# A modulated convolution chain on one core: VectorE's order in the first three quads is rearranged

## The chip, the cores and the metric

The kernel runs on one core of one Trainium2 chip. The metric is the device time of one execution in microseconds (us). In the profile PE is TensorE's matmul, PEld its weight load, DVE VectorE, ACT ScalarE, POOL GpSimd and SP SyncE, which issues most DMAs.

## The reference

The input x has 128 samples of 64 channels by 1024 positions; each sample has a style vector of 128. Four layers follow each other, with weights that depend on the sample, and x is added to the result:

```python
def _layer(x, style, w, b, mw, mb, typ):
    s = style @ mw.T + mb
    weight = SCALE * w * s[:, None, :, None]
    demod = lax.rsqrt(jnp.sum(weight * weight, axis=(2, 3)) + EPS)
    weight = weight * demod[:, :, None, None]
    if typ == 'same':          # 3-tap convolution
        out = jax.vmap(_conv_same)(x, weight) + b[None, :, None]
    elif typ == 'upsample':    # transposed convolution, stride 2, then a 4-tap blur
        out = jax.vmap(_conv_up)(x, weight.transpose(0, 2, 1, 3)) + b[None, :, None]
        out = _blur(out, 2.0 * blur_k, (1, 1))
    elif typ == 'downsample':  # 4-tap blur, then a convolution with stride 2
        xb = _blur(x, blur_k, (2, 2))
        out = jax.vmap(_conv_down)(xb, weight) + b[None, :, None]
    return out
...
for i, typ in enumerate(('same', 'upsample', 'same', 'downsample')):
    out = _layer(out, style, weights[i], biases[i], mod_w[i], mod_b[i], typ)
return x + out
```

No layer has a nonlinearity, so for each sample the four layers are one linear map of x plus a constant, apart from a few positions at both ends.

## The kernel before, in words

The kernel makes use of that. Four samples form a quad, and there are 32 quads. For each quad it first multiplies the layers' weights together and then convolves x with the product.

The weights of a quad pass through four steps on TensorE: `scale3` (ScalarE) and `stage1` (psS, L374) combine two layers, `stage2` (psR, L444) brings in the blur, `stage3` (psW, L485) the first layer. In the loop `stage1` is cut into `stage1_a` and `stage1_b`; `stage1_b` ends with VectorE at L427 and POOL at L430, which both write S. The result W is copied out of PSUM by ScalarE (L345), in the setup partly by VectorE (L347, the constant `BOTH`). `combine_a` and `combine_b` then make the sums H of W (L506) and add the residual to W (L503), all on VectorE.

The convolution itself is a fast convolution: five products, m = 0 to 4, of transformed inputs with transformed weights, each a group of 24 matmuls of 340 columns (`product`, L598). The inputs are made from x by VectorE and POOL, for a quad q:

- `in3` makes T3 from X (L556); `in_g01` and `in_g2` make the two parts of G from X (both L506, G01 with 1376 elements a row and G2 with 684), and after `in_g2` the buffer of X is free, so `load(q + 2)` follows and starts the DMA of quad q + 2 on SyncE's queue.
- `in1` and `in2` make T1 and T2 from G (L571, L576). They take the engine as an argument: in the loop it is POOL.
- `in04` makes T04 from G (L585). There is a single buffer of G, so the next quad's `in_g01` must come behind `in1`, `in2` and `in04` of this one.

The products are `conv3`, `conv1`, `conv2` and `conv0`, all in one PSUM tile psA, and `conv4` in the tile Y. `conv3` starts the bank; ScalarE copies it (`copy_m3`, L630). After `conv1`, VectorE's `sum1` makes y from psA (L506); `conv2` adds to the same bank and so waits for `sum1`. After `conv2`, `sum2` writes Y (L506) and y (L649), and `conv4` adds to Y, `conv0` to psA. ScalarE writes the three outputs (L667) and SyncE stores them.

A constant term runs beside this: `const_first(l)` is a small matmul into Y (L753), `const_rest(l)` turns it into cc or oc on VectorE (L765 to L770) for the next one.

Nothing schedules this kernel: the program is under a manual schedule, so each engine executes its instructions in the order in which the code issues them, and waits by semaphores for what it reads. The order around the change is written out by hand: a setup part for quads 0 and 1, and then a loop over q in which, with n = q + 1 and c = q + 2, the convolution of quad n starts, that of quad q ends, and the inputs of quad c are prepared (`in3(c)`, `in_g01(c)`, `in_g2(c)`, `load(c + 2)`, then `in1(c)`, `in2(c)` on POOL). A sample of the loop before, without what stands between:

```python
combine_a(n); combine_b(n); conv4(q)
...
in04(n); in3(c); in_g01(c)
...
in_g2(c); load(c + NX); extra(q, 1); sum1(n)
...
in1(c, nc_g); in2(c, nc_g); extra(q, 2)
```

`extra` runs small pieces of setup that belong to given quads; `slot` gives small matmuls a place in TensorE's queue.

Of the kernel before, what the change touches and what calls it, by code (L numbers as in the profile page):

```python
# [63 lines left out]
def kernel(  # L64
# [12 lines left out]
    NQ = B // 4  # L77
# [47 lines left out]
    NX = 2  # L125
# [77 lines left out]
    def mod_by_layer(bs, src, dst, f):  # L203

        for l in range(NL):
            nc_a.activation(
                dst[:, l, bs], by_layer(src, bs)[:, l], f, bias=mbs[:, l : l + 1], scale=SCALE
            )
# [255 lines left out]
    def stage3(q, part, pool=None, engs=(nc_a, nc_a)):  # L464

        rt = chain[q]
        ps = unit(pool or ps_w, f"psW{q}_{part}")
        if part == 0:
            Wq[q] = (
                wf_pool.tile([P, 2, K, K, C], F32, tag="Wf", name=f"Wf{q}"),  # L470
                wf_pool.tile([P, 3, 2, K, C], F32, tag="H", name=f"H{q}"),
            )
        W = Wq[q][0]
        kinds = ((0, 1), (2,))[part]
        n = 0
        for i, kind in enumerate(kinds):
            for k in range(K):
                gs = [g for g in range(K) if 0 <= K * g + kind - k < 7]
                lo, m = gs[0], len(gs)
                first = K * lo + kind - k  # L480
                n += 1
                for r, rows in enumerate(HALF):
                    for c, cols in enumerate(HALF):
                        at = (K * i + lo) * C
                        nc.tensor.matmul(  # L485
                            ps[r][cols, at : at + m * C],
                            w0s[kind][rows, k, :],
                            rt[c][rows, first : first + K * (m - 1) + 1 : K, :],
                            start=(n == 1),
                            stop=(n == K * len(kinds)),  # L490
                            skip_group_check=True,
                        )
        for r in range(2):
            dst = W[:, r, kinds[0] : kinds[-1] + 1].rearrange("c t g o -> c (t g o)")
            scaled_copy(engs[r], dst, ps[r][:, : len(kinds) * K * C], t0[:, q, r : r + 1])
        return ps
# [56 lines left out]
    def in3(q, pairs=BOTH_PAIRS):  # L553
        if q < NQ:
            X, t = Xs[q % NX], t_tile(q, "T3")
            nc_v.tensor_sub(t[:, pairs, 0, :NJ], plane(X, 3, pairs), plane(X, 1, pairs))  # L556

    def in_g01(q, pairs=BOTH_PAIRS):
        if q < NQ:
            X, g = g_tile(q)  # L560
            sum_of(g[:, pairs, PL:], X[:, pairs, : 2 * PL], 0.5, X[:, pairs, PL:], ALU.subtract)

    def in_g2(q, pairs=BOTH_PAIRS):
        if q < NQ:
            X, g = g_tile(q)
            sum_of(plane(g, 2, pairs), plane(X, 3, pairs), 0.5, plane(X, 2, pairs), ALU.subtract)
# [65 lines left out]
    def conv1(q, *groups):  # L632
        product(q, 1, banks(q), groups or range(K))

    def sum1(q):

        y1w[q] = m_tile("y1", q, 2)
        for s, a in parts(q):
            sum_of(y1w[q][:, s], a, 2.0, m3c[q][:, s])
# [14 lines left out]
    def conv0(q, *groups):  # L654
        product(q, 0, banks(q), groups)
# [85 lines left out]
    def const_of(l, bs):  # L741

        n = bs.stop - bs.start
        at = NB + 4 + l * n
        return Y[:, 0, at : at + n]
# [4 lines left out]
    def const_first(l, bs):  # L750
        src = c0f if l == 0 else cc[l - 1]
        for cols in HALF:
            nc.tensor.matmul(  # L753
                const_of(l, bs)[cols],
                wsum[T, l, :],
                src[T, bs],
                start=False,
                stop=True,
                skip_group_check=True,
            )  # L760

    def const_rest(l, bs, src):
        src = src[:, : bs.stop - bs.start]
        if l == 2:
            nc_v.tensor_mul(oc[:, bs], src, dm[:, 3, bs])  # L765
            nc_v.tensor_scalar(oc[:, bs], oc[:, bs], bb[:, 3:4], None, op0=ALU.add)
        else:
            add, f = ((b1s, 2.0), (c2f, 1.0))[l]
            nc_v.tensor_mul(cc[l][:, bs], src, (a1, Da)[l][:, bs])
            nc_v.scalar_tensor_tensor(  # L770
                cc[l][:, bs], add[:, bs], f, cc[l][:, bs], op0=ALU.mult, op1=ALU.add
            )
# [221 lines left out]
    weight_sums(1, 2)  # L994
    stage1(1, ps_conv)
    in_g01(0, PAIR[1])
    stage3(0, 0, None, BOTH)
    in3(0)
    stage3(0, 1, ps_conv, BOTH)
    const_first(0, first)  # L1000
    stage1(2)
# [8 lines left out]
    stage2(1, ps_conv)  # L1010
    conv3(0)
    copy_m3(0)
    const_first(1, PART[0])
    in04(0)
    const_rest(1, PART[0], const_of(1, PART[0]))
    stage3(1, 0)
    mod_by_layer(LATER, raw[0][:, 0], sc, AF.Identity)
    in3(1)
    conv1(0)
    in_g01(1, PAIR[0])  # L1020
    in_g01(1, PAIR[1])
    const_first(2, PART[0])
    sum1(0)
    const_rest(2, PART[0], const_of(2, PART[0]))
    in_g2(1)
    load(1 + NX)
    table_b(first)
    in1(1, nc_g)
    in2(1, nc_g)
    for of in (table_B, vector_a1, table_0, vector_b1, vector_c2):  # L1030
        of(PART[1])
    table_Bn(slice(0, PART[1].stop))
# [71 lines left out]
    for q in range(NQ):  # L1104
        n, c, s = q + 1, q + 2, q + 3
        if q == 1:
            nc.sync.dma_start(Xe, x_ends)
        if n == NQ:
            for i, queue in enumerate((nc.sync, nc_a)):
                output(q, 1, i, nc_v)  # L1110
                store(q, i, slice(1, 2), queue)
            conv4(q)
            for i in range(2):
                output(q, 2, i)
                store(q, i, slice(2, K))
            conv0(q, *range(K))
            for i, (eng, queue) in enumerate(zip(BOTH, (nc_a, nc.sync))):
                output(q, 0, i, eng)
                store(q, i, slice(0, 1), queue)
            break  # L1120
        if c < NQ:
            stage2(c)
        if n < NQ - 1:
            sum2(q)
        if n < NQ - 1:
            combine_a(n)
            combine_b(n)

        if n == NQ - 1:

            conv3(n, ps_w)
            copy_m3(n)
            conv4(q, 0, 1)
            for i in range(2):
                output(q, 1, i)
            conv1(n)
            sum1(n)
            conv4(q, 2)
            for i in range(2):
                output(q, 2, i)  # L1140
                store(q, i, slice(1, K))
            in04(n, PAIR[0])
            in04(n, PAIR[1])
            conv0(q, 0)
            conv2(n)
            conv0(q, 1, 2)
            sum2(n)
            for i in range(2):
                output(q, 0, i)
                store(q, i, slice(0, 1))  # L1150
            continue

        conv4(q)
        if q == 0:
            var_matmul(PART[1], var_of(PART[1]), start=False)
            var_root(PART[1], var_of(PART[1]))
            var_newton(PART[1])
            table_A(PART[1], dm[:, 2, PART[1]])
            for of in (table_C, vector_c0, table_3, vector_Da):
                of(PART[1])  # L1160
        for i in range(2):
            output(q, 2, i)
        if c < NQ:
            stage3(c, 0)
        conv3(n)
        copy_m3(n)
        extra(q, 0)
        in04(n)
        in3(c)
        in_g01(c)  # L1170
        if c < NQ:
            stage3(c, 1)
        conv0(q, 0)
        conv1(n, 0)
        if q in SLOTS:
            slot(*SLOTS[q])
        elif s < NQ:
            stage1_a(s)
        conv1(n, 1, 2)
        for i in range(2):  # L1180
            output(q, 1, i)
        in_g2(c)
        load(c + NX)
        extra(q, 1)
        if n == NQ - 2:
            combine_a(n + 1, lambda: sum1(n))
            combine_b(n + 1)
        else:
            sum1(n)
        conv0(q, 1)  # L1190
        if q in SLOTS:
            stage1_a(s)
        elif s < NQ:
            stage1_b(s)
        conv0(q, 2)
        for i in range(2):
            output(q, 0, i)
        conv2(n, 0)
        if q in SLOTS:
            stage1_b(s)  # L1200
        if c < NQ - 1:
            in1(c, nc_g)
            in2(c, nc_g)
        extra(q, 2)
        if s + 1 < NQ:
            scale3(s + 1)
        conv2(n, 1, 2)
        if n == NQ - 2:
            sum2(n)
            in1(n + 1, nc_v)  # L1210
            in2(n + 1, nc_v)
        for i in range(2):
            store(q, i)
# [74 lines left out]
```

## Time and profile before

| What | us |
|---|---|
| median of 3 timed runs | 488.8 |
| lowest and highest of them | 488.52, 490.86 |
| the profiled execution, its own time | 488.43 |
| span of its trace | 486.6 |
| TensorE matmul busy | 478.0 |
| VectorE busy | 381.0 |
| ScalarE busy | 289.9 |
| GpSimd busy | 140.8 |

The span runs from the first to the last instruction of the trace; the execution's own time holds 1.83 us more. Times within the trace count from the start of the span. The loop's first iteration begins at about 33 us, its second at 48 us, and one iteration takes 14 to 15 us. A row of the timeline gives the start, the duration, the engine, the line, the operation, the tile written and the tiles read, and how many instructions are merged; brackets at its end give how long the engine stood idle before it, and what ended that.

### The profile page before, as it was taken

The numbers are of one execution on the slowest core, as the hardware profiler recorded it, in microseconds if no ns is written. First come the engines' busy times: TensorE is split into PE (matmuls) and PEld (weight loads), VectorE is DVE, ScalarE is ACT, GpSimd is POOL, SyncE is SP. The second block draws the span as 40 slices with busy tenths as digits, with TensorE's granted clock in tenths as the row PEclk, the third lists the DMA queues.
The fourth block names the chain that finished last, engine by engine and source line by source line (L and its number), as shares of the span: only waits on it lengthen the run. The fifth ranks groups of instructions, "written<-read, shape, count | busy, mean of one in ns | idle before, by whom it ended". The sixth has DMA issues, their size and how long they took to land.

```text
span 486.6 us, 22180 instructions
## 1 busy us (share of the span) xinstructions
PE 478.0 (98%) x10048; PEld 366.9 (75%) x10048; DVE 381.0 (78%) x630; ACT 289.9 (60%) x579; POOL 140.8 (29%) x173
## 2 busy tenths in 40 slices
PE   8979999999999999999999999999999999999996
PEld 7957777767777777778887877768887777888863
DVE  4787887887798868977867988758888786988784
ACT  5447556666656656656656556656656666556553
POOL 2448035432325333113322123322123331213300
PEclk9989999999999999999999999999999999999999
DMA  7132534444334543344542344442344542244224
GB/s 246 48 145 74 196 128 177 175 157 154 104 118 172 176 176 106 111 153 160 175 166 68 123 173 176 175 141 73 140 175 175 176 173 102 98 174 175 90 87 174
DMA packets 20303, 70.42 MB, mean 145 GB/s; under 512 B 2288, under 2 KB 3824, under 8 KB 20208
## 3 DMA queue, kind: packets, MB, share of 16 engines
q1 hardware_dynamic: 19840, 68.53, 39.4%
q8 instruction: 79, 1.29, 1.0%
q10 hardware_dynamic: 368, 0.46, 0.3%
q14 instruction: 16, 0.13, 0.1%
HBM read 35.36 MB, written 33.62 MB: 142 GB/s over the span
## 4 chain that ended last, share of the span: by engine, by line
PE 96%; DVE 3%; issue 0%; DVEq 0%
PE psA L598 45%; PE psR L444 16%; PE psW L485 14%; PE Y L598 11%; PE psS L374 5%; PE psE L829 2%; PE Y L169 1%; PE Y L321 1%; DVE G L506 1%; DVE H L506 0%; PE psM L193 0%; DVE T L585 0%; DVE T L556 0%; DVE Wf L347 0%; DVE T L571 0%
## 5 line engine op out<-in xcount | busy, mean ns | idle before, releaser
L598 PE MATMUL psA<-T,H 64*64 64x340 f32 x2304 | 193.9, 448 | 2.1 <-DVE y L506 2.0
L598 PEld LDWEIGHTS psA<-T,H 64*64 64x64 f32 x2304 | 96.2, 133 | 51.9 <-issue 13.6
L430 POOL TENSOR_TENSOR S<-S 128x128 f32<-128x128 f32 x29 | 13.7, 471 | 290.9 <-ACT S L345 290.9
L444 PE MATMUL psR<-S,E 64*64 64x192 f32 (+1 forms) x2304 | 87.3, 300 | 0.0
L444 PEld LDWEIGHTS psR<-S,E 64*64 64x64 f32 x2304 | 81.1, 134 | 7.4 <-issue 0.6
L345 ACT ACTIVATE R<-psR,tC 128x448 f32<-128x448 f32 x63 | 36.5, 630 | 72.7 <-PE psR L444 72.7
L506 DVE SCALAR_TENSOR_TENSOR G<-X 128x1376 f32<-128x1376 f32 (+2 forms) x66 | 76.2, 1193 | 0.0
L598 PE MATMUL psA<-T,Wf 64*64 64x340 f32 x768 | 74.7, 447 | 0.0
L345 ACT ACTIVATE Wf<-psW,t 128x384 f32<-128x384 f32 (+1 forms) x126 | 56.3, 497 | 10.9 <-PE psW L485 10.8
L485 PE MATMUL psW<-R,w0s 64*64 64x128 f32 (+1 forms) x1536 | 61.8, 287 | 0.0
L598 PE MATMUL Y<-T,Wf 64*64 64x340 f32 x768 | 61.7, 446 | 0.1
L506 DVE SCALAR_TENSOR_TENSOR Y<-m,psA 128x680 f32<-128x680 f32 (+1 forms) x33 | 28.0, 850 | 37.2 <-PE psA L598 36.7
L485 PEld LDWEIGHTS psW<-R,w0s 64*64 64x64 f32 x1536 | 51.5, 133 | 6.7
L585 DVE TENSOR_TENSOR T<-G 128x1368 f32<-128x1368 f32 (+1 forms) x33 | 50.8, 1542 | 0.1
L506 DVE SCALAR_TENSOR_TENSOR y<-psA,m 128x680 f32<-128x680 f32 (+1 forms) x33 | 27.8, 844 | 28.9 <-PE psA L598 28.4
L667 ACT ACTIVATE o<-Y,tb,td 128x340 f32<-128x340 f32 x64 | 37.1, 630 | 21.4 <-ACT R L345 16.8
L571 POOL TENSOR_TENSOR T<-G 128x684 f32<-128x684 f32 x30 | 49.8, 1660 | 0.1
L576 POOL TENSOR_TENSOR T<-G 128x684 f32<-128x684 f32 x30 | 49.5, 1650 | 0.0
L374 PEld LDWEIGHTS psS<-wd,w2n 64*64 64x64 f32 x1160 | 39.4, 133 | 10.0
L667 ACT ACTIVATE o<-psA,tb,td 128x340 f32<-128x340 f32 x63 | 36.6, 633 | 14.7 <-PE psA L598 14.7
L598 PEld LDWEIGHTS Y<-T,Wf 64*64 64x64 f32 x768 | 33.6, 133 | 14.8 <-issue 0.6
L506 DVE SCALAR_TENSOR_TENSOR H<-Wf 128x384 f32<-128x384 f32 x64 | 39.6, 619 | 0.0
(145 smaller groups left out, 524.5 us busy)
## 6 DMA issues: line engine op xcount, KB each, us to landing
X<-in_x SPq DMA_DIRECT2D x64, 516.0 KB, 4.4
out<-o SPq DMA_DIRECT2D x60, 510.0 KB, 5.3
out<-o SPq DMA_DIRECT2D x6, 170.0 KB, 3.2
out<-o SPq DMA_DIRECT2D x2, 340.0 KB, 2.9
Xe<-in_x_ends SPq DMA_DIRECT2D x1, 512.0 KB, 6.8
par<-in_params SPq DMA_DIRECT2D x2, 192.0 KB, 3.3
out<-o ACTq DMA_DIRECT2D x2, 170.0 KB, 2.6
par_s<-in_params_s SPq DMA_DIRECT2D x1, 196.0 KB, 2.7
```

Source lines behind the costliest of these rows:

```text
L345: nc_a.activation(dst, src, AF.Copy, scale=f)
L374: nc.tensor.matmul(ps[r][cols, at * C : (at + n) * C], weight[rows], wd[c if r == 0 else 1 - c][rows, taps], start=first, stop=last, skip_ ...
L430: nc_g.tensor_add(t[:, :, 2], t[:, :, 2], t[:, :, 0])
L444: nc.tensor.matmul(ps[r][cols, lo * C : (lo + m) * C], E[rows, e + 2, :], src[rows, a, :], start=(n == 0), stop=(n == 8), skip_group_check ...
L485: nc.tensor.matmul(ps[r][cols, at : at + m * C], w0s[kind][rows, k, :], rt[c][rows, first : first + K * (m - 1) + 1 : K, :], start=(n == 1 ...
L506: nc_v.scalar_tensor_tensor(out, x, f, y, op0=ALU.mult, op1=op)
L571: eng.tensor_add(t[:, :, 0, :NJ], plane(g, 2), plane(g, 1))
L576: eng.tensor_sub(t[:, :, 1, :NJ], plane(g, 2), plane(g, 1))
L585: nc_v.tensor_sub(t[:, pairs, :, :NJ], both(a, PL), both(b, 1))
L598: nc.tensor.matmul(ps[s][cols, :NB], w, Ts[q, tag][rows, c, i, g : g + NB], start=(g == 0 and m == 3), stop=(g == K - 1), skip_group_check ...
L667: nc_a.activation(dst, src, AF.Identity, bias=add, scale=d3)
L829: nc.tensor.matmul(ps[r][cols, : HB * n].rearrange("c (b j) -> c b j", j=n), weight(i, r, c)[rows], moving(i, r, c)[rows], start=(i == 0), ...
```

## The change

Only the order in which instructions are issued changes, and the engine of four of them; every sum and every matmul stays. In the setup `in3(0)` moves ahead of `stage3(0, 0)`, and so ahead of VectorE's part in copying W of quad 0; `const_rest(1)` moves ahead of `in04(0)`; `sum1(0)` moves ahead of `in3(1)` and `in_g01(1)`, which is issued for both pairs at once in place of two halves. `in_g2(1)` and `load(3)` move into the first iteration of the loop, behind `combine_b(1)`. In the first iteration `in1(1)` and `in2(1)` run on VectorE ahead of `in04(1)`; `in3(2)` moves behind `sum1(1)`, and `in_g01(2)` behind `stage1_b(3)`. In the second iteration `in_g2(2)` and `load(4)` come ahead of `combine_a(2)`, `in1(2)` and `in2(2)` run on VectorE ahead of `in04(2)`, and `in_g2(3)` and `load(5)` move behind `stage1_b(4)`, with `in1(3)` and `in2(3)` on POOL as before. From the third iteration on the order is the old one.

```diff
     in_g01(0, PAIR[1])
+    in3(0)
     stage3(0, 0, None, BOTH)
-    in3(0)
     stage3(0, 1, ps_conv, BOTH)
...
-    const_first(1, PART[0])
+    const_first(1, first)
+    const_rest(1, first, const_of(1, first))
     in04(0)
-    const_rest(1, PART[0], const_of(1, PART[0]))
     stage3(1, 0)
     mod_by_layer(LATER, raw[0][:, 0], sc, AF.Identity)
+    conv1(0)
+    const_first(2, first)
+    sum1(0)
     in3(1)
-    conv1(0)
-    in_g01(1, PAIR[0])
-    in_g01(1, PAIR[1])
-    const_first(2, PART[0])
-    sum1(0)
-    const_rest(2, PART[0], const_of(2, PART[0]))
-    in_g2(1)
-    load(1 + NX)
+    const_rest(2, first, const_of(2, first))
+    in_g01(1)
     table_b(first)
-    in1(1, nc_g)
-    in2(1, nc_g)
...
         if n < NQ - 1:
+            if q == 1:
+                in_g2(n)
+                load(n + NX)
             combine_a(n)
             combine_b(n)
+            if q == 0:
+                in_g2(n)
+                load(n + NX)
...
+        if q < 2:
+            in1(n, nc_v)
+            in2(n, nc_v)
         for i in range(2):
             output(q, 2, i)
...
         in04(n)
-        in3(c)
-        in_g01(c)
+        if q:
+            in3(c)
+            in_g01(c)
...
-        in_g2(c)
-        load(c + NX)
+        if q > 1:
+            in_g2(c)
+            load(c + NX)
         extra(q, 1)
...
             sum1(n)
+        if q == 0:
+            in3(c)
         conv0(q, 1)
...
             stage1_b(s)
-        if c < NQ - 1:
+        if q == 0:
+            in_g01(c)
+        if q == 1:
+            in_g2(c)
+            load(c + NX)
+        if q and c < NQ - 1:
             in1(c, nc_g)
             in2(c, nc_g)
         extra(q, 2)
```

## The prediction

> **What bounds the kernel now.** I read the page first, then what ended TensorE's waits, then the stretches in which TensorE is not full, then the instructions there.
>
> ```profile
> span 486.6 us, 22180 instructions
> PE 478.0 (98%) x10048; PEld 366.9 (75%) x10048; DVE 381.0 (78%) x630; ACT 289.9 (60%) x579; POOL 140.8 (29%) x173
> PE 96%; DVE 3%; issue 0%; DVEq 0%
> PE psA L598 <- DVE y L506: 2.0, 1, 2.0
> PE Y L753 <- DVE cc L770: 0.6, 1, 0.6
> ```
>
> TensorE is busy for 478.0 of 486.6 us and the chain that ended last is 96% its own. No order of VectorE's work can shorten the matmuls. What such an order can change is TensorE's waits, and the last two rows are the only ones after the start that VectorE causes: 2.0 us for y (`sum1`) and 0.6 us for cc (`const_rest`). The next rows show that these two cost more than their length. Columns: stretch, its length, then busy time of PE, PEld, DVE, ACT and POOL, and the granted clock third from the end.
>
> ```profile
> 24.11:27.53 3.42, 2.81 (x64) 1.64 (x59) 3.32 (x6) 2.16 (x6) 0.00 (x0) 1.00 0.56 223
> 27.53:30.94 3.41, 1.45 (x34) 0.84 (x29) 3.38 (x7) 2.68 (x8) 0.37 (x1) 1.00 0.03 7
> 30.94:34.36 3.42, 3.42 (x44) 2.09 (x40) 1.46 (x3) 0.06 (x1) 3.26 (x4) 0.50 0.58 181
> ```
>
> From 30.94 to 34.36 TensorE never stops, but it has half its clock, so 3.42 us there hold 1.71 us of work. The stretch before it, of the same length, was only 1.45 us busy; the one before that, 2.81 us busy with the 0.6 us wait in it, was followed by full clock. I therefore read the half clock as the second cost of the 2.0 us wait. Together: 0.6 + 2.0 + 1.7, some 4.3 us, is all that there is to gain.
>
> The instructions around the two waits (start, duration, engine, line):
>
> ```profile
> 17.16 0.62 DVE L347 TENSOR_SCALAR Wf<-psW,t 128x384 f32<-128x384 f32 x1 [1.82 <-PE psW L485]
> 21.82 0.87 DVE L571 TENSOR_TENSOR T<-G 128x684 f32<-128x684 f32 x1
> 24.26 0.86 DVE L576 TENSOR_TENSOR T<-G 128x684 f32<-128x684 f32 x1
> 25.04 1.57 DVE L585 TENSOR_TENSOR T<-G 128x1368 f32<-128x1368 f32 x1
> 25.77 0.74 PE L598 MATMUL psA<-T,H 64*64 64x340 f32 x8
> 26.54 0.17 DVE L769 TENSOR_TENSOR cc<-Y,Da 128x16 f32<-128x16 f32 x1
> 26.91 0.87 DVE L556 TENSOR_TENSOR T<-X 128x684 f32<-128x684 f32 x1
> 27.13 0.23 PE L753 MATMUL Y<-cc,wsum 64*64 64x16 f32 x2 [0.61 <-DVE cc L770]
> 27.24 0.99 PE L485 MATMUL psW<-R,w0s 64*64 64x128 f32 x22
> 27.70 1.65 DVE L506 SCALAR_TENSOR_TENSOR G<-X 128x688 f32<-128x688 f32 x2
> 29.27 0.86 DVE L506 SCALAR_TENSOR_TENSOR y<-psA,m 128x680 f32<-128x680 f32 x1
> 30.18 2.99 PE L598 MATMUL psA<-T,H 64*64 64x340 f32 x24 [1.96 <-DVE y L506]
> 31.74 1.63 POOL L571 TENSOR_TENSOR T<-G 128x684 f32<-128x684 f32 x1
> 33.22 0.87 DVE L506 SCALAR_TENSOR_TENSOR Y<-m,psA 128x680 f32<-128x680 f32 x1 [1.96 <-PE psA L598]
> 34.77 0.61 DVE L506 SCALAR_TENSOR_TENSOR H<-Wf 128x384 f32<-128x384 f32 x1
> 36.13 1.90 PE L598 MATMUL Y<-T,Wf 64*64 64x340 f32 x24
> 38.83 0.22 DVE L234 TENSOR_SCALAR var<-Y 128x64 f32<-128x64 f32 x1 [0.78 <-ACT dm L233]
> 40.24 1.60 DVE L585 TENSOR_TENSOR T<-G 128x1368 f32<-128x1368 f32 x1
> 42.80 0.82 PE L598 MATMUL psA<-T,H 64*64 64x340 f32 x8
> ```
>
> `conv1(0)` ends at 25.77 + 0.74 = 26.51, so `sum1(0)` could start there. VectorE starts it at 29.27, because T04(0), cc, T3(1) and both halves of G01(1) stand ahead. `conv2(0)` writes the bank that `sum1(0)` reads and starts at 30.18, 0.05 after y is done. (T1, T2, T3, T04 are outputs of `in1`, `in2`, `in3`, `in04`; G01 and G2 of `in_g01`, `in_g2`.)
>
> **Part by part.** In the built program the queues of TensorE and ScalarE keep their order; VectorE gets four instructions that POOL loses (T1 and T2 of quads 1 and 2). So TensorE's pieces keep their lengths, and it is enough to run VectorE's new queue against them.
>
> T3(0) ahead of the copy of W: 0.87 us go into the 1.82 us in which VectorE waits for that copy's matmuls. Cost nothing; at 17.8 the next copy follows at once, and everything up to T2(0) moves up by about 0.67 us. TensorE is full until 26.51, so this gains nothing by itself; without that idle time it would cost nothing there either, as the old place cost the same.
>
> cc of quad 1 ahead of T04(0): T2(0) now starts at 24.26 - 0.67 = 23.59, cc is done near 24.8, before TensorE asks at 26.5. The 0.61 us wait goes. What is late next: T04(0) runs 24.85 to 26.42, and its readers come after 36 in the old run.
>
> `sum1(0)` ahead of T3(1) and G01(1): it starts when `conv1(0)` ends, 26.55, and ends at 27.41; `conv2(0)` starts at 27.46. The piece before it, psW, ended at 27.24 + 0.99 = 28.23 and is now 0.61 earlier, 27.62, its last matmul overlapping the next by about 0.2: no wait is left, or one of 0.1. So `conv2(0)` moves from 30.18 to 27.46, **2.72 us**. With full clock, 1.71 us more until the matmuls into Y: 36.13 becomes 31.70, a shift of **4.43 us**.
>
> Now what was put off. VectorE starts its next instruction about 0.08 before an independent one ends (T04 at 25.04 with 1.57, then cc at 26.54), so T3, T1, T2 and G2 take 0.78 each, G01 1.51. From `sum1(0)` at 26.55: 0.79, T3(1) 0.78, the two constants 0.35, G01(1) 1.51 reach 29.98, where `sum2(0)` begins; `conv2(0)` is done at 29.2, so that is 0.8 late, but its reader needs Y at 31.70 and it is there at 30.85. Y and y take 1.55 (33.22 to 34.77), H near 3.2 (3.11 between two rows of quad 1 below, a little more here), G2(1) 0.78: 35.5. Variances and the table take 1.41 (38.83 to 40.24): 36.94. T1(1) then ends at 37.81 on VectorE. Its first matmuls, at 42.80, are due at 38.37: 0.56 to spare, the thinnest cover in quad 0; if it is gone, its lack is the price, bounded by the 0.78 of T1. T2(1) and T04(1) end at 40.07, and `sum1(1)` must wait for its matmuls until 41.04.
>
> The load of quad 3 follows G2(1), so it is issued at 35.6, and it is needed at the T3(3) near 53: no price. Loads 4 and 5 are read later still.
>
> Quad 1 has the tightest stretch, from `sum1(1)` to `sum1(2)`:
>
> ```profile
> 45.47 0.87 DVE L506 SCALAR_TENSOR_TENSOR y<-psA,m 128x680 f32<-128x680 f32 x1 [0.53 <-PE psA L598]
> 46.26 0.61 DVE L427 SCALAR_TENSOR_TENSOR S<-psS,tB,S 128x128 f32<-128x128 f32 x2
> 48.49 0.87 DVE L506 SCALAR_TENSOR_TENSOR Y<-m,psA 128x680 f32<-128x680 f32 x1 [1.63 <-PE psA L598]
> 50.05 0.55 DVE L506 SCALAR_TENSOR_TENSOR H<-Wf 128x384 f32<-128x384 f32 x1
> 53.16 1.58 DVE L585 TENSOR_TENSOR T<-G 128x1368 f32<-128x1368 f32 x1
> 54.65 0.87 DVE L556 TENSOR_TENSOR T<-X 128x684 f32<-128x684 f32 x1
> 55.43 2.37 DVE L506 SCALAR_TENSOR_TENSOR G<-X 128x1376 f32<-128x1376 f32 x2
> 58.10 0.17 DVE L769 TENSOR_TENSOR cc<-raw,a 128x16 f32<-128x16 f32 x1 [0.30 <-ACT raw L688]
> 59.11 0.87 DVE L506 SCALAR_TENSOR_TENSOR y<-psA,m 128x680 f32<-128x680 f32 x1 [0.63 <-PE psA L598]
> 60.52 0.79 PE L598 MATMUL psA<-T,H 64*64 64x340 f32 x8
> ```
>
> Before, this stretch held waits of 1.63, 0.30 and 0.63 us. After, VectorE has no pause in it: y 0.79, T3(2) 0.78, S 0.53, G01(2) 1.51, Y and y 1.56, G2(2) 0.78, H 3.11 (50.05 to 53.16), T1(2) and T2(2) 1.56, T04(2) 1.49, T3(3) 0.78, G01(3) 1.51, cc 0.39: 14.79, then y 0.87 and the 0.05 of release, 15.71. TensorE reaches `conv2(2, 0)` 60.52 - 45.47 = 15.05 after `sum1(1)` starts, and that matmul overwrites what `sum1(2)` reads. So a **new wait of 0.66 us** stands there. Within the stretch S is done 0.6 before its reader and H in time; T1(2) ends near 51.0, due at 52.6. Afterwards G2(3) is behind S and is covered by the wait for S; quad 2 ends this backlog in its own slack, and from quad 3 on the order is the old one.
>
> T1 and T2 on VectorE are priced by 0.87 of the row at 21.82, the same operation on VectorE; the other bound is POOL's 1.63. I take 0.87, the engine's own row.
>
> Sum: 2.72 + 1.71 - 0.66 = 3.77 us. The profiled execution took 488.43 for its 486.6 of span and becomes 484.66; the median of the three timed runs is 0.37 above it, so I forecast 488.8 - 3.8 = 485.0.
>
> One rule bears on the 1.71. The half clock lasted 3.42 us after a stretch that was 1.45 of 3.41 busy and whose longest pause was 1.96. The Trainium skill, "TensorE: Matmul & The Clock Gate", in Part 1 and in "HAM oscillation", has the clock halve after at least one idle window of about 3.4 us, and advises against idle gaps above that; the length agrees with the trace, but here 1.96 us of pause was already followed by half clock. By the page's gap rule the wait would not be the cause, and the half clock could stay.
>
> **Rivals.** *The half clock stays, or comes back in quad 1.* For it: only one such event is in the trace, so its threshold lies anywhere between 1.45 and 2.81 busy us. Against it: with a pause of 0.66 at least 2.75 of 3.41 us are busy, next to the 2.81 that was harmless. It would leave 2.72 - 0.66 = 2.06: 486.7 us. The gap rule of the page gives this rival.
>
> *VectorE becomes the bound in quad 1, and the kernel is slower.* Its stretch of 15.71 us has no pause, so whatever stretches its instructions lengthens TensorE's wait one for one. At 2 us more the wait is 2.7, longer than the one that preceded the half clock; 1.71 follows, and the 4.43 is used up: that is the point of decision. With T1 and T2 at POOL's price (+0.78 each) and the five H operations as slow as this one was while POOL worked beside it (+0.34 each), it is 0.66 + 3.26 + 1.71, and some 0.35 in quad 0: 6.0 lost against 4.43, 490.4 us.
>
> ```profile
> 64.31 0.89 DVE L506 SCALAR_TENSOR_TENSOR H<-Wf 128x384 f32<-128x384 f32 x1
> ```
>
> Against it: VectorE's own T1 row, and POOL has little to do in that stretch once T1(2) and T2(2) are gone.
>
> *The change hides everything:* VectorE a little quicker than summed, no wait in quad 1: 4.4 saved, 484.4 us. It is the good end of the forecast and needs 0.66 us out of 15.71.
>
> **How the numbers follow.** No change, for a measurement of this kernel, is within 0.5%, 2.4 us. The forecast with its good end gets 0.80, all of it faster. The half clock that stays saves 2.06, under the bound, and with other half-losses that I cannot name gets 0.14. The slower rival gets 0.06. The range runs from 483.8 (the good end, less 0.6, somewhat more than the 0.37 by which two figures of the kernel before differ) to 487.0 (the half clock that stays, and 0.3): it leaves out little more than the slower rival.
>
> **What would show it.** In the changed profile: no wait for cc or y near 27 to 30, `conv2(0)` near 27.5, granted clock 1.00 from 27 to 38, TensorE's Y matmuls of quad 0 at 31.7, T1(1) on VectorE done near 37.8, one wait of TensorE for y of 0.3 to 1.2 us near 56, and from there the old timeline 3.8 us earlier. I am wrong if the clock is still 0.50 somewhere before 60, if TensorE waits for T or S in quad 0, or if the wait in quad 1 is above 1.5 us.

## The result, and the profile after

| | before | changed |
|---|---|---|
| median, us | 488.62 (7 runs) | 486.01 (7 runs) |
| lowest to highest, us | 487.43 to 490.86 | 485.38 to 486.75 |
| ratio of changed to before | | 0.9945, 95% interval 0.9926 to 0.9964 |

The changed kernel is 2.6 us faster (1.8 to 3.6 by the interval); 3.8 were forecast. The profiled execution took 486.4 us, its span is 484.6.

From the page of the changed kernel:

```profile
span 484.6 us, 22175 instructions
PE 476.6 (98%) x10048; PEld 373.4 (77%) x10048; DVE 384.6 (79%) x633; ACT 289.8 (60%) x579; POOL 133.9 (28%) x169
PE 91%; DVE 6%; DMA 1%; issue 0%; ACT 0%; DVEq 0%; ACTq 0%
```

What TensorE waited for in it (total, times, longest):

```profile
PE Y L169 <- DVE Z L142: 1.2, 1, 1.2
PE psA L598 <- DVE y L506: 0.7, 2, 0.5
```

The wait for cc is gone, and in place of one wait of 2.0 us for y there are two of 0.7 together. The chain shows more VectorE than before: from 22.5 to 57.7 us, in quads 0 and 1, VectorE now has one pause above 0.2 us, of 1.82 us ahead of `sum1(1)`.

The same stretches as before, with the granted clock third from the end:

```profile
24.11:27.53 3.42, 3.36 (x77) 2.46 (x68) 3.32 (x6) 2.18 (x7) 0.00 (x0) 1.00 0.56 226
27.53:30.94 3.41, 3.25 (x68) 2.40 (x72) 3.38 (x6) 2.72 (x8) 1.92 (x3) 1.00 0.01 2
30.94:34.36 3.42, 3.42 (x84) 2.57 (x80) 3.35 (x8) 1.21 (x3) 2.20 (x8) 1.00 0.02 5
```

TensorE is nearly full in all three, and there is no half clock. Its pieces, one row for each place where the prediction gave a time:

```profile
27.69 1.95 PE L598 MATMUL psA<-T,H 64*64 64x340 f32 x24 [0.22 <-DVE y L506]
...
31.95 1.90 PE L598 MATMUL Y<-T,Wf 64*64 64x340 f32 x24
...
35.58 1.97 PE L598 MATMUL psA<-T,H 64*64 64x340 f32 x24
37.67 1.29 PE L485 MATMUL psW<-R,w0s 64*64 64x128 f32 x22
...
39.32 0.94 PE L598 MATMUL psA<-T,H 64*64 64x340 f32 x8
...
57.71 0.80 PE L598 MATMUL psA<-T,H 64*64 64x340 f32 x8 [0.46 <-DVE y L506]
```

| start of | before | forecast | after | shift |
|---|---|---|---|---|
| `conv2(0)` | 30.18 | 27.46 | 27.69 | -2.49 |
| `conv4(0)` | 36.13 | 31.70 | 31.95 | -4.18 |
| `conv1(1, 0)` | 42.80 | 38.37 | 39.32 | -3.48 |
| `conv2(2, 0)` | 60.52 | 56.75 | 57.71 | -2.81 |

So 4.18 us were won by the matmuls into Y, a little under the forecast; 0.70 were lost between `conv4(0)` and `conv1(1, 0)`, which the prediction does not have; and 0.67 in quad 1, which it has as 0.66. From there on the two timelines keep a distance of 2.8 us (matmuls into psR at 207.54 and 204.73), and of 3.0 at the start of the last group of matmuls (480.13 and 477.13). What follows that group, the last stores, took about 1 us longer in this execution, so the span shows 2.0.

Where the 0.70 went: ScalarE, VectorE and the weight loads of the changed kernel near 36 us.

```profile
35.68 0.22 DVE L234 TENSOR_SCALAR var<-Y 128x64 f32<-128x64 f32 x1
...
35.99 1.16 ACT L667 ACTIVATE o<-Y,tb,td 128x340 f32<-128x340 f32 x2 [1.37 <-DVE var L234]
...
37.04 1.05 ACT L345 ACTIVATE Wf<-psW,t 128x384 f32<-128x384 f32 x2
...
37.67 0.20 PEld L485 LDWEIGHTS psW<-R,w0s 64*64 64x64 f32 x4 [0.72 <-ACT Wf L345]
```

ScalarE's first output waits 1.37 us for L234, a small VectorE instruction that reads the variances from the same bank of Y. Behind the output in ScalarE's queue stands the copy of W, and TensorE's next weights wait for that. In the kernel before the same output had waited 0.35 us for L234:

```profile
39.15 1.16 ACT L667 ACTIVATE o<-Y,tb,td 128x340 f32<-128x340 f32 x2 [0.35 <-DVE var L234]
```

The output uses nothing that L234 writes, so the wait is not for its result. The Trainium skill, "PSUM — Partial Sum Buffer", in "PSUM bank collisions raise a hardware error", says that ScalarE and VectorE must not read the same bank and quadrant at once, and that such accesses are put in an order; that fits the wait, and no run here tries it without.

### The profile page after: what moved, and what is told of

Its sections match the earlier page's. It is cut to its first block, busy times and chain, and to the rows that moved or that the text cites. A ratio compares the mean times of both kernels' runs of the same rounds, so it can differ in the third digit from the quotient of the medians.

```text
span 484.6 us, 22175 instructions
## 1 busy us (share of the span) xinstructions
PE 476.6 (98%) x10048; PEld 373.4 (77%) x10048; DVE 384.6 (79%) x633; ACT 289.8 (60%) x579; POOL 133.9 (28%) x169
## 4 chain that ended last, share of the span: by engine, by line
PE 91%; DVE 6%; DMA 1%; issue 0%; ACT 0%; DVEq 0%; ACTq 0%
PE psA L598 43%; PE psR L444 15%; PE psW L485 14%; PE Y L598 11%; PE psS L374 5%; PE psE L829 2%; DVE H L506 1%; DVE G L506 1%; DMA par_s<-in_params_s 1%; DVE T L585 1%; PE Y L321 1%; DVE T L556 0%; PE psM L193 0%; DVE T L571 0%; DVE T L576 0%
## 5 line engine op out<-in xcount | busy, mean ns | idle before, releaser
L598 PEld LDWEIGHTS psA<-T,H 64*64 64x64 f32 x2304 | 99.7, 133 | 47.1 <-issue 12.3
L506 DVE SCALAR_TENSOR_TENSOR G<-X 128x684 f32<-128x684 f32 (+1 forms) x65 | 76.1, 1206 | 0.0
L485 PE MATMUL psW<-R,w0s 64*64 64x128 f32 (+1 forms) x1536 | 62.8, 287 | 0.2
L485 PEld LDWEIGHTS psW<-R,w0s 64*64 64x64 f32 x1536 | 52.5, 133 | 6.8 <-ACT Wf L345 1.0
L571 POOL TENSOR_TENSOR T<-G 128x684 f32<-128x684 f32 x28 | 46.5, 1659 | 2.3 <-DVE G L506 2.3
L576 POOL TENSOR_TENSOR T<-G 128x684 f32<-128x684 f32 x28 | 46.5, 1661 | 0.0
L598 PEld LDWEIGHTS Y<-T,Wf 64*64 64x64 f32 x768 | 34.9, 133 | 13.7 <-issue 0.6
L345 ACT ACTIVATE S<-psS,tBn 128x256 f32<-128x256 f32 x58 | 24.3, 470 | 25.2 <-PE psS L374 25.1
```

The costliest lines, as they stand in the source:

```text
L345: nc_a.activation(dst, src, AF.Copy, scale=f)
L485: nc.tensor.matmul(ps[r][cols, at : at + m * C], w0s[kind][rows, k, :], rt[c][rows, first : first + K * (m - 1) + 1 : K, :], start=(n == 1 ...
L506: nc_v.scalar_tensor_tensor(out, x, f, y, op0=ALU.mult, op1=op)
L571: eng.tensor_add(t[:, :, 0, :NJ], plane(g, 2), plane(g, 1))
L576: eng.tensor_sub(t[:, :, 1, :NJ], plane(g, 2), plane(g, 1))
L598: nc.tensor.matmul(ps[s][cols, :NB], w, Ts[q, tag][rows, c, i, g : g + NB], start=(g == 0 and m == 3), stop=(g == K - 1), skip_group_check ...
```

## The experiments

All times are medians; each group was compared with the kernel before on the same chip, 488.65 us for the first four and 488.62 for the others. Gains over the changed kernel are against its 486.01, which was not run again beside the experiments; the kernel before, which was, gave nearly the same median each time. Where two such times lie close, the trace decides.

**1. The variances ahead of G2(1).**

```diff
-            if q == 0:
-                in_g2(n)
-                load(n + NX)
...
             table_A(PART[1], dm[:, 2, PART[1]])
+            in_g2(n)
+            load(n + NX)
```

> The changed kernel with G2(1) and load(3) put behind the variances of quads 4 to 7 (L234 and its Newton step) on VectorE, nothing else. Theory: ScalarE's first output of quad 0 waits for VectorE's L234, which reads the same bank of Y, and through it the copy of W and TensorE's second part of stage3(2) are late; L234 then starts near 34.9 instead of 35.7 and the output near 35.2 instead of 36.0, TensorE's conv1(1, 0) starts some 0.7 us earlier than at 39.3, and the kernel is about 0.7 us faster than the changed one (3.3 us faster than the kernel before). Rival: the output waits for its table tb or for the matmuls into Y; then it stays at 36.0 and the time is that of the changed kernel.

Measured: 485.43 us, ratio to before 0.9939 (0.9923 to 0.9956). ScalarE and TensorE in its trace:

```profile
35.24 1.16 ACT L667 ACTIVATE o<-Y,tb,td 128x340 f32<-128x340 f32 x2 [0.58 <-DVE var L234]
...
38.74 0.78 PE L598 MATMUL psA<-T,H 64*64 64x340 f32 x8
```

The output starts at 35.24 for 35.99, `conv1(1, 0)` at 38.74 for 39.32, and the median falls by 0.58. The intervals of this kernel and of the changed one overlap, so the time alone would not show it, but the trace has the same 0.58. The output follows L234, so this is 0.58 of the 0.70, shown by moving one VectorE instruction with its load; the output still waits 0.58 us for L234, which stands behind the H operations.

**2. T1(2) and T2(2) on POOL.**

```diff
         if q < 2:
-            in1(n, nc_v)
-            in2(n, nc_v)
+            in1(n, (nc_v, nc_g)[q])
+            in2(n, (nc_v, nc_g)[q])
```

> The changed kernel with T1(2) and T2(2) on POOL again, 1.56 us less of VectorE's work between sum1(1) and sum1(2). Theory (VectorE's queue sets the wait of TensorE for y in quad 1): that wait of 0.46 us goes, with what is lost around it some 0.67 us, VectorE waits for TensorE before sum1(2) instead, and the kernel is 0.6 to 0.7 us faster than the changed one. Rival (POOL's adds disturb VectorE's sums beside them, and G01(3) must wait for POOL's T2(2)): VectorE gains less than 1 us, a wait stays, and the time is within 0.3 us of the changed kernel.

Measured: 487.61 us, 0.998 (0.9969 to 0.9991): 1.6 us slower than the changed kernel. Both expectations fall short; the rival had the right engine and far too small a size. Its timeline, VectorE, POOL and TensorE:

```profile
48.09 0.55 DVE L506 SCALAR_TENSOR_TENSOR H<-Wf 128x384 f32<-128x384 f32 x1
48.32 1.83 POOL L571 TENSOR_TENSOR T<-G 128x684 f32<-128x684 f32 x1 [6.00 <-DVE G L506]
48.56 3.27 DVE L503 SCALAR_TENSOR_TENSOR Wf<-idn,t,Wf 128x64 f32<-128x64 f32 x2
...
50.12 1.63 POOL L576 TENSOR_TENSOR T<-G 128x684 f32<-128x684 f32 x1
...
52.48 1.95 PE L598 MATMUL psA<-T,H 64*64 64x340 f32 x24 [1.58 <-DVE H L506]
```

The two residual instructions take 0.47 us in the changed kernel (48.46) and 3.27 here: they end when POOL's second addition ends, at 51.75. So 1.56 us of work less cost VectorE 2.8 us of standing still, and H was late for `conv3(2)`.

**3. Only the part ahead of the loop.** The edit is the first block of the diff above, with `in_g2(1)`, `load(3)` and T1(1), T2(1) on POOL left in the setup, and the loop of the kernel before.

> Only the part of the change that lies ahead of the loop: T3(0) in the wait for W, cc of quad 1 ahead of T04(0), sum1(0) ahead of T3(1) and G01(1); G2(1), load(3), T1(1) and T2(1) on POOL stay in the setup and the loop is that of the kernel before. Theory: the whole gain comes from here: the waits for cc and y and the half clock go, conv4(0) starts near 32, the wait for L234 stays (0.7 us) but the new wait in quad 1 does not come: 3.3 to 3.6 us faster than the kernel before, 0.6 to 0.8 faster than the change as a whole. Rival: without the loop's part VectorE is late in quad 0 (G2(1) ahead of sum2(0), T3(2) and G01(2) ahead of sum1(1)), TensorE waits there for 0.5 us or more, and it is no faster than the change as a whole.

Measured: 487.23 us, 0.9981 (0.9967 to 0.9995). The theory is wrong here, and the rival is right that TensorE waits in quad 0, with a larger loss than it gave, but not in the cause that it named: `sum2(0)` was done at 31.88, before its reader at 32.02, and VectorE had 1.92 us to spare before `sum1(1)`. Its timeline:

```profile
32.88 1.96 POOL L576 TENSOR_TENSOR T<-G 128x684 f32<-128x684 f32 x1
33.27 1.85 DVE L503 SCALAR_TENSOR_TENSOR Wf<-idn,t,Wf 128x64 f32<-128x64 f32 x2
...
37.60 1.16 ACT L667 ACTIVATE o<-Y,tb,td 128x340 f32<-128x340 f32 x2 [2.92 <-DVE var L234]
...
39.28 1.83 PE L485 MATMUL psW<-R,w0s 64*64 64x128 f32 x22 [1.57 <-ACT Wf L345]
```

and the stretch behind that, with its granted clock:

```profile
39.90:43.30 3.40, 3.40 (x39) 2.82 (x38) 3.40 (x4) 1.24 (x3) 3.27 (x4) 0.50 0.02 5
```

POOL's T2(1) now runs beside quad 1's residual, which stands still again, 1.85 us for 0.47. L234 is at 37.28, 1.60 later than in the changed kernel, and 1.38 of that is the residual. ScalarE's output comes behind it, TensorE waits 1.57 us for the copy of W, and half clock follows. So T1 and T2 on VectorE are not a price paid for nothing: they keep POOL out of the stretch that the earlier `sum1(0)` has filled. This is read from the trace; no run has the setup's part with T1(1) and T2(1) alone moved to VectorE.

**4. A wait of 1.8 us put back before `conv2(0)`.**

```diff
     const_first(2, first)
+    in3(1)
+    in_g01(1, PAIR[0])
     sum1(0)
-    in3(1)
     const_rest(2, first, const_of(2, first))
-    in_g01(1)
+    in_g01(1, PAIR[1])
```

> The changed kernel with T3(1) and the first half of G01(1) ahead of sum1(0) again, so that TensorE waits for y for some 1.8 us before conv2(0), without the earlier wait for cc. If the half clock follows from this wait, the granted clock is 0.50 for 3.4 us near 31 and the kernel loses 1.6 + 1.7 = 3.3 us against the changed one, about 0.7 slower than the kernel before or equal to it. If it takes both waits together, or something other than a wait, the clock stays at 1.00 and it loses 1.6 us only.

Measured: 487.74 us, 0.9993 (0.9979 to 1.0007), and neither answer is the whole one. The profiled execution had the wait (timeline):

```profile
29.28 1.95 PE L598 MATMUL psA<-T,H 64*64 64x340 f32 x24 [1.76 <-DVE y L506]
```

and full clock behind it (stretches):

```profile
26.00:29.40 3.40, 1.64 (x44) 1.00 (x40) 3.37 (x6) 2.96 (x12) 0.00 (x0) 1.00 0.05 16
29.40:32.80 3.40, 3.40 (x76) 2.55 (x80) 2.46 (x4) 0.91 (x3) 2.68 (x11) 1.00 0.00 0
```

But its 12 timed executions fall into two groups by the mean clock that each of them lists: five with 0.993 or 0.994 took 488.57 to 489.34 us, seven with 0.997 or 0.998 took 487.03 to 487.74. Their medians, 489.14 and 487.24, are 3.1 and 1.2 us above the changed kernel, near the two losses expected. 3.42 us at half clock are 0.0035 of the mean, about the distance. So such a wait brings the half clock in a part of the executions. The kernel before is alike: of its 48 executions in both groups, 26 list 0.995 or less (median 488.9), 17 list 0.997 or more (median 487.6), five lie between. The changed kernel and experiments 1, 2, 5, 6 and 8 list 0.996 or more throughout.

**5. T3(0) back behind the copy of W.**

```diff
-    in3(0)
     stage3(0, 0, None, BOTH)
+    in3(0)
```

> The changed kernel with T3(0) behind VectorE's copy of the first part of W again, as in the kernel before. Theory (VectorE's next copy, of W's second part, waits for ScalarE's copy out of the same bank until 18.17 in any case, so T3(0) ahead of it brings VectorE some 0.1 us and not 0.67): T2(0) ends within 0.2 us of the changed kernel's, and the time is that of the changed kernel within 0.3 us. Rival (the move is worth its 0.67 us): TensorE's wait for y before conv2(0) grows from 0.22 to some 0.9 us, and the kernel is 0.5 to 0.7 us slower than the changed one.

Measured: 485.98 us, 0.995 (0.9935 to 0.9965): no difference from the changed kernel, as the theory has it. In the changed kernel's timeline the second copy of W waits for ScalarE's copy out of the same tile:

```profile
17.05 0.62 DVE L347 TENSOR_SCALAR Wf<-psW,t 128x384 f32<-128x384 f32 x1 [0.96 <-PE psW L485]
18.17 0.42 DVE L347 TENSOR_SCALAR Wf<-psW,t 128x192 f32<-128x192 f32 x1 [0.50 <-ACT Wf L345]
```

The expectation says bank. In the kernel the two copies read the two halves, of 512 elements each, of one tile of PSUM, so no run shows that the bank is the reason. The first pair of copies reads two tiles and ran side by side (16.98 on ScalarE, 17.05 on VectorE).

**6. Experiment 1, and G01(3) behind `sum1(2)`.**

```diff
         if q:
             in3(c)
+        if q > 1:
             in_g01(c)
...
         if q == 0:
             in3(c)
+        if q == 1:
+            in_g01(c)
         conv0(q, 1)
```

> The changed kernel with the variances ahead of G2(1), as in the first experiment, and with G01(3) behind sum1(2) in quad 1, 1.51 us less of VectorE's work between sum1(1) and sum1(2), with POOL as in the change. Theory (VectorE's own queue makes the wait for y in quad 1, 15.6 us of work against 15.05): that wait goes, VectorE waits for TensorE before sum1(2), and nothing else comes late, as G01(3) runs in the 1.2 us in which VectorE waits for S and some 0.3 beyond: 0.5 to 0.7 us faster than the first experiment, 3.7 to 3.9 faster than the kernel before. Rival (S or sum2(2) becomes late in its place): a wait of TensorE for S near 59 or for Y near 61, and no gain.

Measured: 484.50 us, 0.9915 (0.9901 to 0.993): 0.93 faster than experiment 1, more than the theory has, 1.5 faster than the change, and the fastest kernel here. In the trace 0.60 of the 0.93 lies between `conv1(1, 0)` and `conv2(2, 0)`; where the rest lies is open. What TensorE still waits for behind the start, and quad 1 in its timeline:

```profile
PE psA L598 <- DVE y L506: 0.3, 1, 0.3
```

```profile
55.14 0.87 DVE L506 SCALAR_TENSOR_TENSOR y<-psA,m 128x680 f32<-128x680 f32 x1 [0.33 <-PE psA L598]
55.93 1.58 DVE L506 SCALAR_TENSOR_TENSOR G<-X 128x1376 f32<-128x1376 f32 x1
...
56.54 0.79 PE L598 MATMUL psA<-T,H 64*64 64x340 f32 x8
```

In quad 1 VectorE now waits for TensorE before `sum1(2)` and TensorE no longer for y; the 0.3 left is the wait before `conv2(0)`.

**7. cc ahead of T04(0) alone**, in the kernel before.

```diff
     const_first(1, PART[0])
+    const_rest(1, PART[0], const_of(1, PART[0]))
     in04(0)
-    const_rest(1, PART[0], const_of(1, PART[0]))
```

> The kernel before with cc of quad 1 ahead of T04(0) and nothing else. sum1(0) keeps its place, so conv2(0) still starts near 30.2. Theory (the two waits are not a sum, the later one takes what the earlier gives): TensorE's wait for cc goes, its wait for y grows from 2.0 to 2.6 us, and the time is that of the kernel before within 0.3 us, unless the longer single pause halves the clock in more executions than the 13 to 18 of 29 in which the kernel before showed a mean clock of 0.996 or less, by up to 0.8 us. Rival (each wait counts): 0.6 us faster.

Measured: 488.31 us, 0.9995 (0.9983 to 1.0007): nothing, as the theory has it. TensorE in its timeline:

```profile
30.31 1.79 PE L598 MATMUL psA<-T,H 64*64 64x340 f32 x16 [2.75 <-DVE y L506]
```

The wait for y took over what the wait for cc gave back. The two were in series behind one queue, so only the last of them sets `conv2(0)`.

**8. One more addition on POOL beside `combine(2)`.**

```diff
                 load(n + NX)
+                nc_g.tensor_add(scratch[:, :, :NJ], plane(Gs[n], 2), plane(Gs[n], 1))
             combine_a(n)
```

> The changed kernel with one more addition on POOL that nobody reads: the two planes of G(2) that T1(2) is made of, 684 elements a row, issued behind G2(2), so beside combine(2) on VectorE. Theory (while POOL works through an addition of two operands, VectorE's operations with two operands wait for its end): the two residual instructions of L503 take 1.3 us or more together where they take 0.47 in the changed kernel, and the wait in quad 1 grows by 1.0 to 1.5 us. Rival (what lengthened L503 with T1 and T2 on POOL was something else, such as data that POOL held): L503 stays at 0.47 and the time too.

Measured: 487.04 us, 0.997 (0.9957 to 0.9983), 1.0 slower than the changed kernel. Its timeline:

```profile
48.14 1.89 POOL L1125 TENSOR_TENSOR scratch<-G 128x684 f32<-128x684 f32 x1 [5.93 <-DVE G L506]
48.45 1.87 DVE L503 SCALAR_TENSOR_TENSOR Wf<-idn,t,Wf 128x64 f32<-128x64 f32 x2
```

L503 took 1.87 for 0.47, with nothing else changed and nobody reading POOL's sum; it ends 0.3 after POOL. The theory holds for L503; the wait in quad 1 grew by 0.81 (1.27 for 0.46), a little less than it has. The Trainium skill, "GPSIMD Engine Reference", in "Key points", says that POOL shares its SBUF interfaces with VectorE and that they contend when VectorE reads two SBUF inputs; L503 does, and here the contention is a full stop until POOL's instruction ends.

## Why the prediction was right or wrong

**The bound, and where the gain lies: right.** TensorE's order and pieces stayed, and the whole gain came from its waits between 26 and 31 us and the clock behind them. `conv2(0)` moved by 2.49 where 2.72 was forecast. The time alone would not show it: 486.0 is 1.0 from the forecast of 485.0 and 0.7 from 486.7, the rival in which the half clock stays. The granted clock of 1.00 after the change decides between them. And that the time lies in the range although a wait of 0.70 us is missing from the sum is luck: the range reached up to 487.0 for the sake of that rival.

**T3(0): wrong.** "Everything up to T2(0) moves up by about 0.67 us" failed at "the next copy follows at once": that copy waits for ScalarE's and starts only 0.33 earlier (18.17 for 18.50), and the residual was slower, 0.90 us for 0.47, with one H quicker by 0.22. T2(0) moved by 0.12 (24.26 to 24.14), so T04(0) ended at 26.86, `sum1(0)` began at 26.77 for 26.55, and `conv2(0)` had its 0.22 us of wait. Experiment 5 shows the move to be worth nothing.

**cc and `sum1(0)`: right together.** Experiment 7 shows that cc alone is worth nothing, experiment 4 that the place of `sum1(0)` carries 1.7 of the 2.6 us. The opening sum of 0.6 + 2.0 + 1.7 holds as the time of one stall, not as prices of single edits.

**The clock: mechanism right, size wrong for a median.** Half clock follows such a wait and went with it. But I took 1.71 us, the price in the one profiled execution, for all executions. Something between 26 and 31 of 48 executions of the kernel before had it, so a median holds only a part: the changed kernel's 486.0 is 2.9 us below the ones that surely had it (488.9) and 1.6 below the ones without (487.6).

In experiment 4 a wait of 1.8 us brings it in five executions of twelve. The traces show a grid behind this. In the record of the granted clock that each of them holds, the changes lie whole multiples of 3.413 us apart: 20.48 (six) and 3.41 us in the kernel before, 30.72 (nine) and 3.41 in the third experiment. The grid lies differently against the span each time: the stretch of it that holds the wait is 27.53 to 30.94 in the kernel before, and 26.30 to 29.71 in experiment 4. That fits windows that run free of the kernel, as the Trainium skill, "TensorE: Matmul & The Clock Gate", Part 1, says of them. TensorE's busy time in such a stretch, as the profile has it, does not decide alone: half clock followed on 1.45 us of it in the kernel before and on 1.80 in the third experiment (36.46 to 39.87), and not on 1.65 in experiment 4. So the bound between 1.45 and 2.81 that the prediction looked for is not one number; what does decide is open. The gap rule of the same page of the Trainium skill, in "HAM oscillation", which gave the first rival, is not borne out: single pauses of 1.57, 1.96 and 2.75 us, below its 3.4, were followed by half clock. The rival did not come: 0.22 and 0.46 us of wait left the clock at 1.00.

**Late in quad 0: the step that was missed.** The working put L234 and the Newton step behind G2(1) and costed them only by VectorE's 1.41 us and by T1(1) behind them. "It is enough to run VectorE's new queue against them", TensorE's pieces, left ScalarE's queue out: it did not ask who waits for L234. The row that showed it is the one of the trace of before shown above, a wait of ScalarE's output for L234 of 0.35 us. Experiment 1 wins back 0.58 of the 0.70. TensorE did wait in quad 0, though not for T or S as I had listed, but for ScalarE.

**Quad 1: right.** VectorE's stretch was forecast at 15.71 us; from 42.08 to 57.71 it is 15.63. The new wait cost 0.67, forecast 0.66, and experiment 6 removes it. T1(1) was done at 37.96, forecast 37.81.

**The slower rival** did not come, though its mechanism exists. Operations of VectorE do stand still beside POOL's additions, by more than the 0.34 I gave them: experiments 2, 3 and 8. In the change none of these additions runs in quad 1's stretch, as they moved to VectorE. The 0.34 was misread as a price for each operation. The H at 64.31, from which it came, waited for the end of POOL's instruction:

```profile
63.14 1.64 POOL L576 TENSOR_TENSOR T<-G 128x684 f32<-128x684 f32 x1
```

POOL ends at 64.78 and this H at 65.20, 0.42 behind it. In the changed kernel itself the residual at 62.37, behind the stretch, takes 1.85 us for 0.47 beside POOL's T2(3); it costs nothing there, as TensorE has no wait behind it.

The sum in the trace: 4.18 - 0.70 - 0.67 = 2.81, against 4.43 - 0.66 = 3.77. Of the lack, 0.70 is the missed wait and 0.25 T3(0). The median's 2.6 includes the half clock in only a part of the runs before.

## What to carry to other kernels

When an instruction is moved back in a queue, look for everyone who waits for it, above all another engine that reads the same tile in PSUM; the wait stands in the trace of before, however short. Price a clock drop by the share of executions that list it, not by the one that was profiled. And where two engines share work, moving an addition to the slower engine can cost the faster one more than it gives back.

## What the runs showed of the hardware that was not expected

An addition of 684 elements on POOL stops VectorE's residual, whose two tensors lie in SBUF, until it ends: 0.47 us became 1.87 beside one addition and 3.27 beside two in a row. The trace of the kernel before has the same for H: all 12 of its instructions that began inside such an addition ended 0.41 to 0.42 us behind it, and took 0.61 to 0.95 us for 0.55. L649, which reads one tensor from SBUF and one from PSUM, kept its 0.85 us in all 12 such cases. And the half clock is a matter of chance: 1.76 us of wait gave it in 5 of 12 executions, 1.57 us (quad 0, third experiment) in 4 of 12, and 1.58 us (quad 1, second experiment) in none of 11, which is left open.
